# Row loads of the feed-forward chunks issued by GpSimd, and another order of the buffers in the attention loop's scope

## The chip, the core and the metric

The kernel runs on one core of a Trainium2 chip. A core has five engines that the profile tells apart: PE (TensorE, matrix products; PEld is its loading of weights), DVE (VectorE), ACT (ScalarE), POOL (GpSimd) and SP (SyncE, which only issues transfers). Each engine takes its own instructions in order; engines wait for each other by semaphores. A transfer (DMA) is issued by SP, ACT or POOL and lands later. The metric is the device time of one execution in microseconds; of several runs the median counts. All arithmetic is in float32.

## The reference

The input x is a batch of 4 images of 64 x 64 positions with 256 channels. Two layers follow each other:

```python
x = x + L0_conv(_gn(x), ...)       # deformable sampling: 8 groups x 9 taps, bilinear
t = _to_tokens(x)                  # 4 images of 4096 tokens x 256
t = t + L1_attn(_ln_t(t), ...)     # additive attention inside an image
t = t + L1_ffn(_ln_t(t), ...)      # feed-forward of chosen tokens
```

The attention takes `softmax_k(sum_u Wa[u] * tanh(q[i,u] + k[j,u] + bh))` over 32 units for every pair of the 4096 tokens of an image, and the weighted mean of the tokens with it. The feed-forward chooses tokens by a router and leaves the others as they are:

```python
weights = einsum('bsd,do->bso', x, wr) + br
_, idx = top_k(weights, 2048)
sel_idx = idx[:, :2047]
h = gelu(sel @ w1 + b1)            # 256 -> 1024
y = (h @ w2 + b2) * weights[sel]   # 1024 -> 256
return processed + x               # y set at the chosen tokens, 0 elsewhere
```

## The kernel before

**Stages.** First comes the convolution part of all four images together with the sampling of image 0 (L1518 to L1529, to 1355 us of the profiled execution). Then there is a loop over the images n (L1531). In it one scope of buffers (L1538 to L1541) holds three things beside each other: `feed_forward(n - 1)` of the image before, `attention_prep(n)`, and a part of the sampling of image n + 1. They are generators, and the string `turns` (L1547 to L1552), written by hand, says in which order their steps are emitted: m is a step of the feed-forward, o one of the preparation, s one of the sampler. A second scope (L1559 to L1562) holds `attention(n)`, a loop of 8 blocks of 512 queries by 32 blocks of 128 keys by four head parts, with the rest of the sampling as side work. After the loop, `feed_forward(3)` runs alone (L1567).

**What sets the order.** Instructions wrapped in `keep`, and those emitted through `pinned` (DVE in the loop), stay on their engine in the order of the program. Everything else (ACT, SP, POOL and loads) is placed by a scheduler when the kernel is built. The attention loop's order is written out by hand (L1144 to L1150). A buffer is a tile of a pool; the pools of a scope lie one behind the other in each partition of SBUF in the order in which the scope lists them. A pool that lies where pools of an earlier scope lay has to wait for the users of those.

**The feed-forward** (L1367 to L1502). It loads the tokens as `v`, computes router weights, finds the threshold and gives every token a rank. 32 indirect transfers on POOL (L1423, list `put`) scatter the rows, with four numbers behind each (so 260 floats), in the order of rank to `sort_d` in DRAM. While they run, ACT computes the rows of all tokens as if none were chosen (L1435) and sends them to the output (L1439). Then 2048 ranked rows are taken in four chunks of 512. `chunk(s)` (L1449 to L1474) loads them (`get`, L1455, 512 rows of 1,040 bytes), after all of `put`; DVE makes the row numbers `si` (L1461), ACT normalises (L1463), PE transposes (helper `transpose4`, L903 and L904), POOL adds (L1469) and DVE scales (L1471). The body then runs the first product (`ph`, L1483) with gelu on ACT (L1484), the second product (`py`, L1489), DVE's L1492, and for each 128 rows an indirect scatter on POOL to the output (L1496). `chunk(s + 1)` is called after the second of the four scatters of chunk s. The loaded rows are double-buffered inside the one tile `big` (three parts: hT, two xs, two vs), which lies in pool `one` with the weights w1 and w2; the transposed rows (xT) are in pool `row`.

**The start of the attention loop.** `queries(0)` (L998 to L1004) takes two tiles of pool `qp`: it loads qf from DRAM on SP (L1000), and POOL makes qn from it (L1003). PE multiplies keys with qf (D, L1017) and with qn (N, L1027). ACT takes the logarithm of D into a tile r of pool `rp` (L1111) and its exponential (L1113); DVE multiplies it by N (L1032). POOL and DVE add (L1117 to L1124), ACT makes weights (L1039), and PE multiplies them by the values (L1055) into `acv` of pool `ap` (L1079); the weights are in pool `ep`.

**The sampler.** In the stage beside the feed-forward it loads weights `wb` on SP (L819), and DVE multiplies and adds with them (L828, L838). POOL fetches some exact rows by indirect loads `xre` (L679, L684), which DVE uses (L757).

**The preparation.** For each block of keys, PE and ACT (L951, kf) make the factors of the attention; DVE's step `least` (L969) follows in the same block. PE's last instruction of the preparation is L978, after which the attention loop's D can run.

Of the kernel before, what the change touches and what calls it, by code (L numbers as in the profile page):

```python
# [37 lines left out]
PVB = 8  # L38
# [8 lines left out]
def layers_kernel(ctx: ExitStack, tc: tile.TileContext, a, out: bass.AP):  # L47
    nc = tc.nc
# [192 lines left out]
    @contextmanager  # L241
    def scope(*pools):

        with ExitStack() as st:
            for name, bufs, psum in pools:
                kw = {"space": PSUM} if psum else {}
                setattr(S, name, st.enter_context(tc.tile_pool(name=name, bufs=bufs, **kw)))
            yield
            for name, _, _ in pools:
                delattr(S, name)  # L250
# [612 lines left out]
    def sample_any(n):  # L863

        num = nc.values_load(large[0:1, n : n + 1], min_val=0, max_val=L)
        with tc.If(num > P), scope(
            ("smp", 2, 0), ("two", 2, 0), ("sb", 2, 0), ("dn", 1, 0), ("ps_t", 1, 1), ("ps_m", 1, 1)
        ):
            cur = S.two.tile([P, 1], F32, tag="cur", name="cur")
            nc.vector.tensor_copy(cur, part)  # L870
            with tc.For_i(0, NT, 1):
                exact = []
                for _ in exact_rows(n, cur, exact):
                    pass
                put_rows(n, *exact[0])
                nc.vector.tensor_scalar(cur, cur, float(P), None, ALU.add)
# [21 lines left out]
    def transpose4(dst, src, vec=nc.vector):  # L898

        pt = S.ps_d.tile([P, CC, 512], F32, tag="d", name="ptt")  # L900
        for k in range(CC):
            for t in range(4):
                nc.tensor.transpose(pt[:, k, t * P : (t + 1) * P], src[:, t, k * P : (k + 1) * P], ident)  # L903
        vec.tensor_copy(dst, pt)  # L904
# [462 lines left out]
    def feed_forward(n, vec):  # L1367
# [81 lines left out]
        def chunk(s):  # L1449

            o = nh + s % 2 * nx
            xs = big[:, o : o + nx].rearrange("p (t c) -> p t c", t=4)
            o = nh + 2 * nx + s % 2 * nv
            vs = big[:, o : o + nv].rearrange("p (t c) -> p t c", t=4)
            get = nc.sync.dma_start(  # L1455
                out=xs, in_=sort_d[n][s * 512 : (s + 1) * 512].rearrange("(t p) c -> p t c", p=P)
            )
            for ins in put:
                tc.add_manual_dep(get.ins, ins.name, in_order, reason="rows in order")
            si = S.two.tile([P, 4], I32, tag="si", name="si")  # L1460
            vec.tensor_scalar(si, xs[:, :, C + 3], float(n * L), None, ALU.add)  # L1461
            for t in range(4):
                nc.scalar.activation(  # L1463
                    vs[:, t, :], xs[:, t, :C], AF.Identity, bias=xs[:, t, C + 1 : C + 2], scale=xs[:, t, C : C + 1]
                )
            xT = S.row.tile([P, CC, 512], F32, tag="vT", name="xT")
            transpose4(xT, vs, vec)

            nc.gpsimd.tensor_tensor(vs, vs, xs[:, :, :C], ALU.add)  # L1469
            for t in range(4):  # L1470
                vec.scalar_tensor_tensor(  # L1471
                    vs[:, t, :], b2, xs[:, t, C + 2 : C + 3], vs[:, t, :], ALU.mult, ALU.add
                )
            held[s] = xs, vs, si, xT  # L1474

        chunk(0)
        yield
        for s in range(NSORT // 512):
            xs, vs, si, xT = held.pop(s)
            for f in range(FF // P):  # L1480
                ph = S.ps_m.tile([P, 512], F32, tag="pm", name="ph")
                for k in range(CC):
                    nc.tensor.matmul(ph, w1[:, k, rows(f)], xT[:, k, :], start=(k == 0), stop=(k == CC - 1))  # L1483
                S.tables.append(nc.scalar.activation(hT[:, f, :], ph, AF.Gelu_apprx_tanh, bias=b1[:, f, :]))  # L1484
            yield
            for t in range(4):
                py = S.ps_m.tile([P, C], F32, tag="pm", name="py")
                for f in range(FF // P):
                    nc.tensor.matmul(  # L1489
                        py, hT[:, f, rows(t)], w2[:, f, :], start=(f == 0), stop=(f == FF // P - 1)  # L1490
                    )
                vec.scalar_tensor_tensor(  # L1492
                    vs[:, t, :], py, xs[:, t, C + 2 : C + 3], vs[:, t, :], ALU.mult, ALU.add
                )
                m = min(P, NSEL - s * 512 - t * P)
                nc.gpsimd.indirect_dma_start(  # L1496
                    out=out_rows, out_offset=bass.IndirectOffsetOnAxis(ap=si[:m, t : t + 1], axis=0),
                    in_=vs[:m, t, :], in_offset=None,
                )
                if t == 1 and s + 1 < NSORT // 512:  # L1500
                    chunk(s + 1)
                yield  # L1502
# [28 lines left out]
    for n in range(NB):  # L1531
        with scope(("att", 1, 0), ("smp", 2, 0), ("dn", 1, 0)):
            v = S.att.tile([P, NT, C + 1], F32, name="v")
            kf = S.att.tile([P, 2, L], F32, name="kf")

            sampling = sample_image(n + 1) if n + 1 < NB else iter(())
            S.gather = False
            with scope(  # L1538
                ("one", 1, 0), ("two", 2, 0), ("sb", 2, 0), ("row", 2, 0), ("rp", 3, 0),
                ("ps_d", 2, 1), ("ps_n", 1, 1), ("ps_m", 3, 1),  # L1540
            ):  # L1541


                main = feed_forward(n - 1, pinned) if n else iter(())
                prep = attention_prep(n, v, kf, pinned)
                if n:
                    turns = (  # L1547
                        "mos" + "m" * 3 + "mo" * 8 + "om" + "oss" * 2 + "m" + "oss" * 7 + "m" + "oss" * 3
                        + ("m" + "ossss" * 3 + "msss" * 4) * 4
                    )  # L1550
                else:
                    turns = "o" * 10 + "s" + "os" * 24  # L1552
                for turn in turns:
                    next({"m": main, "o": prep, "s": sampling}[turn], None)
                for rest in (main, prep):
                    for _ in rest:
                        pass
            S.gather = True
            with scope(  # L1559
                ("two", 2, 0), ("sb", 2, 0), ("rp", 6, 0), ("qp", 2, 0),  # L1560
                ("ep", 2 * PVB + 1, 0), ("ap", 1, 0), ("ps_d", 2, 1), ("ps_n", 3, 1), ("ps_m", 1, 1),
            ):  # L1562
                attention(n, v, kf, [sampling])
        attention_any(n)
        if n + 1 < NB:
            sample_any(n + 1)
# [39 lines left out]
```

## Time and profile before

| | |
|---|---|
| median of 5 runs | 10437.7 us (10423.64 to 10448.31) |
| profiled execution: time | 10445.84 us |
| profiled execution: span | 10444.1 us |
| granted TensorE clock, mean | 0.934 |
| first attention loop begins (first L1017) | 1468.81 us |
| stage between the loops of images 0 and 1 | 3456 to 3861 us, 405 |
| stage between the loops of images 1 and 2 | 5766 to 6164 us, 398 |
| stage between the loops of images 2 and 3 (no sampling) | 8070 to 8393 us, 323 |
| feed-forward of image 3, alone | 10177 to 10444.1 us, 267 |
| SP ahead of L1455, all waits: for the scatters (`sort`) | 211.0 us in 11 |
| SP ahead of L1455: for `big` | 92.7 us (L263) and 62.2 us (L1492) |
| first L1455 of the four images | 3629.90, 5933.84, 8220.01, 10307.15 |

The span is the time from the first to the last instruction that the profiler shows; the execution's own time is 1.7 us longer. A line of a view names the engine, the line of the program, the operation, and its output and input by the program's names of tiles. In views of waits, `X L1 <- Y Z: a, b, c` says that engine X ahead of its line L1 waited for Y's work on Z, a us in all, in b waits, of which the longest took c. An engine's name with a q (SPq) means its sequencer, the part that issues. In the order of time a line begins with the start and the duration in us, and the bracket behind it gives the idle time of the engine ahead of that instruction and what ended it. The page's strip of 40 digits shows the busy share of an engine in slices of a fortieth of the span, in tenths. The profile is of one execution; durations below a microsecond vary between instances.

### The profile page before, as it was taken

The numbers are of one execution on the slowest core, as the hardware profiler recorded it, in microseconds if no ns is written. First come the engines' busy times: TensorE is split into PE (matmuls) and PEld (weight loads), VectorE is DVE, ScalarE is ACT, GpSimd is POOL, SyncE is SP. The second block draws the span as 40 slices with busy tenths as digits, with TensorE's granted clock in tenths as the row PEclk, the third lists the DMA queues.
The fourth block names the chain that finished last, engine by engine and source line by source line (L and its number), as shares of the span: only waits on it lengthen the run. The fifth ranks groups of instructions, "written<-read, shape, count | busy, mean of one in ns | idle before, by whom it ended". The sixth has DMA issues, their size and how long they took to land. (4 is left out here: it accounts for less than half of the span.)

```text
span 10444.1 us, 117382 instructions
## 1 busy us (share of the span) xinstructions
PE 9292.6 (89%) x38892; PEld 4517.1 (43%) x38892; DVE 8527.5 (82%) x13743; ACT 7465.7 (71%) x8525; POOL 5226.6 (50%) x3042
## 2 busy tenths in 40 slices
PE   5777779999999589999999589999999699999995
PEld 3444434444444344444444344444444344444443
DVE  5798979898989679899898679899898367777772
ACT  3333348888888338888888358888887389999991
POOL 0231027676555327677655237677555155555552
PEclk9788879999999789999999789999999799999997
DMA  3476632222222342222111442222111300000002
GB/s 106 138 201 188 206 122 64 62 65 61 71 66 72 122 148 54 52 53 56 53 58 44 139 136 54 53 52 55 52 58 39 103 13 8 10 7 7 7 5 76
DMA packets 381592, 766.07 MB, mean 73 GB/s; under 512 B 49361, under 2 KB 212849, under 8 KB 380945
## 3 DMA queue, kind: packets, MB, share of 16 engines
q1 hardware_dynamic: 290448, 608.84, 18.8%
q0 software_dynamic: 30144, 45.87, 3.0%
q10 hardware_dynamic: 60352, 103.50, 2.8%
q8 instruction: 312, 5.11, 0.2%
q14 instruction: 336, 2.74, 0.1%
HBM read 580.88 MB, written 177.14 MB: 73 GB/s over the span
## 5 line engine op out<-in xcount | busy, mean ns | idle before, releaser
L1032 DVE TENSOR_TENSOR r<-nn,r 128x512 f32<-128x512 f32 x6144 | 3937.7, 681 | 874.1 <-PE nn L1027 819.3
L1027 PE MATMUL nn<-qn,kf 32*128 32x512 f32 (+1 forms) x12288 | 4518.0, 640 | 133.9 <-DVE r L1032 97.3
L1117 POOL TENSOR_TENSOR r<-r 128x1024 f32<-128x1024 f32 x1024 | 2708.7, 2645 | 2647.8 <-DVE r L1032 2637.9
L1111 ACT ACTIVATE r<-d 128x1024 f32<-128x1024 f32 x3072 | 3114.0, 1014 | 1095.0 <-DVE r L1121 701.5
L1017 PE MATMUL d<-qf,kf 32*128 32x512 f32 (+1 forms) x12288 | 3340.3, 632 | 76.5 <-DMA qf<-qf 43.1
L1113 ACT ACTIVATE r<-r 128x1024 f32<-128x1024 f32 x3072 | 3124.1, 1051 | 32.7
L1027 PEld LDWEIGHTS nn<-qn,kf 32*128 32x128 f32 (+1 forms) x12288 | 1400.0, 185 | 1898.4 <-DVE r L1032 1448.3
L1055 PE MATMUL pv<-v,et 128*128 128x257 f32 x8192 | 2116.5, 402 | 14.8 <-DVE acv L1079 14.8
L1055 PEld LDWEIGHTS pv<-v,et 128*128 128x128 f32 x8192 | 1516.0, 195 | 981.4 <-issue 771.5
L1017 PEld LDWEIGHTS d<-qf,kf 32*128 32x128 f32 (+1 forms) x12288 | 1018.2, 186 | 1340.3 <-issue 725.6
L1119 POOL TENSOR_TENSOR r<-r 128x512 f32<-128x512 f32 x1024 | 1331.7, 1300 | 99.4 <-DVE r L1032 24.3
L828 DVE TENSOR_TENSOR prd<-xs,wb 128x1024 f32<-128x1024 f32 x768 | 978.0, 1273 | 90.6 <-DMA wb<-wt 83.8
L838 DVE TENSOR_TENSOR ac<-ac,prd 128x1024 f32<-128x1024 f32 x768 | 993.3, 1293 | 6.6
L724 POOL DMA_INDIRECT ga<-tab,tii x576 | 701.5, 1218 | 348.9 <-DVE so L738 203.4
L1039 ACT ACTIVATE et<-et,nshift 128x512 f32<-128x512 f32 x1024 | 723.7, 707 | 29.6 <-DVE et L1124 29.6
L1121 DVE TENSOR_TENSOR r<-r 128x512 f32<-128x512 f32 x1024 | 719.7, 703 | 4.1 <-POOL r L1117 3.7
L1124 DVE TENSOR_TENSOR et<-r 128x512 f32<-128x512 f32 x1024 | 695.6, 679 | 0.4
L263 PE MATMUL pc<-xn,diag 128*128 128x512 f32 x1008 | 449.2, 601 | 21.4 <-ACT xn L397 8.3
L788 POOL TENSOR_TENSOR xr<-xr,outb 128x512 f32<-128x512 f32 x64 | 87.1, 1367 | 551.5 <-DMA xr<-in_x_dram 551.4
L263 PE MATMUL ptc<-ident,xp 128*128 128x128 f32 (+1 forms) x576 | 136.0, 349 | 207.4 <-ACT tb L456 206.2
L263 PEld LDWEIGHTS pc<-xn,diag 128*128 128x128 f32 x1008 | 190.7, 192 | 255.6 <-issue 221.7
L456 ACT COPY tb<-ptc 128x256 f32<-128x256 f32 (+1 forms) x288 | 104.4, 370 | 240.5 <-PE ptc L263 131.0
(342 smaller groups left out, 5253.5 us busy)
## 6 DMA issues: line engine op xcount, KB each, us to landing
wb<-wt SPq DMA_DIRECT2D x800, 512.0 KB
tab<-tb ACTq DMA_DIRECT2D x128, 256.0 KB
v<-t SPq DMA_DIRECT2D x64, 512.0 KB
xs<-xp SPq DMA_DIRECT2D x32, 680.0 KB
xp<-xp ACTq DMA_DIRECT2D x32, 544.0 KB
xt<-in_x_dram SPq DMA_DIRECT2D x32, 512.0 KB
xr<-in_x_dram SPq DMA_DIRECT2D x64, 256.0 KB
t<-xr SPq DMA_DIRECT2D x64, 256.0 KB
```

Source lines behind the costliest of these rows:

```text
L263: return lambda *args, **kw: keep(op(*args, **kw))
L828: keep(nc.vector.tensor_tensor(pr.rearrange("p (r w) -> p r w", w=W), src, wb.rearrange("p (r w) -> p r w", w=W), ALU.mult,))
L838: keep(nc.vector.tensor_add(ac[:, f, :], ac[:, f, :], pr))
L1017: keep(nc.tensor.matmul(d[:, j, :], kf[g, blk, rows(kt)], qs[q][0][g, blk, :], start=True, stop=True))
L1027: keep(nc.tensor.matmul(nn, kf[g, blk, rows(kt)], qs[q][1][g, blk, :], start=True, stop=True))
L1032: keep(nc.vector.tensor_tensor(r[:, j, :], ns[j], r[:, j, :], ALU.mult))
L1039: keep(nc.scalar.activation(ets[b], ets[b], AF.Exp, bias=nshift))
L1055: keep(nc.tensor.matmul(pv, ets[b0 + i][:, rows(j)], v[:, k0 + i, :], start=(i == 0), stop=(i == PVB - 1)))
L1111: keep(nc.scalar.activation(rs[b, p], ds.pop((b, p)), AF.Ln))
L1113: keep(nc.scalar.activation(rs[b, p], rs[b, p], AF.Exp, scale=-1.0))
L1117: keep(nc.gpsimd.tensor_tensor(rs[b, 1], rs[b, 1], rs[b, 2], ALU.add))
L1119: keep(nc.gpsimd.tensor_tensor(rs[b, 1][:, 0], rs[b, 1][:, 0], rs[b, 3][:, 0], ALU.add))
```

## The change

Two edits. The load of the ranked rows of each chunk, L1455, is issued by GpSimd in place of SyncE: 16 loads in the whole program, four for each image. And the scope of the attention loop lists its pools in another order: `ep` comes straight after `sb`, `rp` after it, then `ap`, and `qp` last of the pools in SBUF; before, it was `rp`, `qp`, `ep`, `ap`. Their sizes are as before, and the pools of PSUM (`ps_d`, `ps_n`, `ps_m`) are not touched.

```diff
@@ -1452,7 +1452,7 @@
             xs = big[:, o : o + nx].rearrange("p (t c) -> p t c", t=4)
             o = nh + 2 * nx + s % 2 * nv
             vs = big[:, o : o + nv].rearrange("p (t c) -> p t c", t=4)
-            get = nc.sync.dma_start(
+            get = nc.gpsimd.dma_start(
                 out=xs, in_=sort_d[n][s * 512 : (s + 1) * 512].rearrange("(t p) c -> p t c", p=P)
             )
             for ins in put:
@@ -1557,8 +1557,8 @@
                         pass
             S.gather = True
             with scope(
-                ("two", 2, 0), ("sb", 2, 0), ("rp", 6, 0), ("qp", 2, 0),
-                ("ep", 2 * PVB + 1, 0), ("ap", 1, 0), ("ps_d", 2, 1), ("ps_n", 3, 1), ("ps_m", 1, 1),
+                ("two", 2, 0), ("sb", 2, 0), ("ep", 2 * PVB + 1, 0), ("rp", 6, 0), ("ap", 1, 0), ("qp", 2, 0),
+                ("ps_d", 2, 1), ("ps_n", 3, 1), ("ps_m", 1, 1),
             ):
                 attention(n, v, kf, [sampling])
         attention_any(n)
```

## The prediction

> **What bounds the kernel now.** I read the page first, then busy times by stage, then the waits inside the stages that the change touches, then the order in time.
>
> ```profile
> span 10444.1 us, 117382 instructions
> PE 9292.6 (89%) x38892; PEld 4517.1 (43%) x38892; DVE 8527.5 (82%) x13743; ACT 7465.7 (71%) x8525; POOL 5226.6 (50%) x3042
> PE   5777779999999589999999589999999699999995
> DVE  5798979898989679899898679899898367777772
> ```
>
> PE and DVE are full in four long plateaus, the attention loops. Between them lie four stages that are not full: feed-forward of one image beside the preparation of the next (images 1, 2, 3 of the loop over images, counted from 0), and the last feed-forward alone. The change touches only these. The busy times by stage (length; then PE, PEld, DVE, ACT, POOL) show the first one and the last one:
>
> ```profile
> 3456.00:3861.00 405.00, 248.62 (x816) 154.54 (x816) 272.00 (x537) 105.18 (x152) 84.51 (x66) 0.76 0.51 163
> 10177.00:10444.10 267.10, 150.16 (x540) 101.59 (x536) 73.35 (x258) 54.52 (x89) 63.10 (x56) 0.77 0.22 74
> ```
>
> No engine is full there, so waits set their length: 405 + 398 + 323 + 267 = 1393 us of 10444, the most that is in question. Two waits are the change's subject. The first, in the waits of SP and of all engines from 3596 to 3650 us (total, times, longest):
>
> ```profile
> SPq L1455 <- DMA sort<-v,rif: 29.9, 3, 27.5
> ACT big L1463 <- DMA big<-sort: 31.0, 2, 30.4
> DVE prd L828 <- DMA wb<-wt: 29.1, 3, 27.5
> ```
>
> The 32 scatters of L1423 run to 3628.1 (32 x 1.264 us from 3585.25). Chunk 0's load L1455 stands in SP's queue until they have landed (3629.90), and the sampler's wb loads stand behind it, so DVE idles 27.5 us for wb. Beside it ACT idles 30.4 us for the same rows: its next instruction is chunk 0's L1463. Image 2 repeats this (28.5 and 32.3 us).
>
> The second, in order of time at the start of image 1's loop:
>
> ```profile
> 3846.22 2.55 POOL L1496 DMA_INDIRECT out_dram<-big,si  x1 [4.42 <-DMA out_dram<-big,si]
> ...
> 3856.43 0.55 SPq L1000 DMA_DIRECT2D qf<-qf  x1
> ...
> 3857.13 1.00 POOL L684 DMA_INDIRECT xre<-in_x_dram,rii  x1 [8.36 <-DMA out_dram<-big,si]
> ...
> 3860.58 2.09 PE L1017 MATMUL d<-qf,kf 32*128 32x512 f32 x8 [13.61 <-DMA qf<-qf]
> ...
> 3862.82 1.94 ACT L1111 ACTIVATE r<-d 128x1024 f32<-128x1024 f32 x2 [52.69 <-PE d L1017]
> ...
> 3863.97 0.42 DVE L757 TENSOR_TENSOR tte<-xre,outb 128x256 f32<-128x256 f32 x1 [16.45 <-ACT r L1111]
> ...
> 3868.14 1.29 DVE L1032 TENSOR_TENSOR r<-nn,r 128x512 f32<-128x512 f32 x2 [2.37 <-PE nn L1027]
> ```
>
> The last scatter of the feed-forward lands 10 us after its issue. Only then does SP load qf (3856.43), PE multiply (3860.58), ACT start (3862.82), DVE follow (3868.14). A look at L1111 alone shows that ACT has a wait of its own that ends at the same landing, 3856.3, and a later one for d, 3862.7:
>
> ```profile
> L1111 ACTq EVENT_SEMAPHORE x2: 38/3216/6394, 3856.3 to 3862.7; - x2
> ```
>
> **Part 1, qp last in the scope.** It adds no instruction; it moves buffers. Bytes per partition in images 1 and 2, from where both scopes start: the feed-forward's `one` takes 0 to 54,240, `sb` ends at 73,312, `row` at 81,504, `rp` at 93,792. The loop's qp lies at 36,992 to 53,376 before (inside `one`, over w1 and w2) and at 75,920 to 92,304 after (over `row` and `rp`). That qf waits for the scatters though it overlaps w1 alone shows that a buffer waits for every user of a pool that it overlaps. In its new place it waits for the last L1483 (done 3808) and the qe stores (last issued 3799.4), so qf is loaded some 40 us early, and d of the first key block is in PSUM when PE has done L978 (3846.97). The two qn products of L1003 (1.57 us each) move ahead too; POOL has holes of 3.7 to 4.6 us between L1496, which hide them. Image 3 has the same overlaps.
>
> What is late next: the six r buffers of rp move to 47,232 to 71,808, still over the end of `one`, so L1111 keeps its wait to 3856.3. It gains 3862.82 - 3856.5 = 6.3 us, not 14. In images 1 and 2 DVE has L757 ahead of L1032. If L757 stayed at 3863.97, L1032 would start when L838 ends, 3865.8, and gain 2.3 us (2.0 in image 2). xre landed 6.8 us after its issue with two 512 KB qf loads beside it; indirect rows land in a median of 2.6. Without those loads I take 5 us, between 2 and 6.3. Image 3 has no L757: its landing is 8388.4, L1111 8394.86, so 6.3. Image 0 has no wait (qf loaded at 1415.6, d follows L978 at once): 0. **Sum 16.3 us, between 10.6 and 18.9.**
>
> **Part 2, the 16 loads on POOL.** Removed from SP: 16 issues of 0.37 us and the waits ahead of them. Added to POOL: the same issues and waits. POOL has nothing of use to do between the last L1423 and L1469 (20 us idle), so its own waiting for the rows costs nothing in chunks 0 and 1.
>
> Gain: wb flows, and DVE takes up L828 at 3608 instead of 3635.8. It does not win 27.5 us. After 7.7 us of work (3635.81 to 3643.53) it stands at `least`, which needs ACT's kf (L951), and ACT still stands at chunk 0's rows. From these, ACT's next four groups take 2.07 + 1.00 + 2.08 + 1.02 = 6.2 us, so `least` starts at 3633.78 + 6.3 = 3640.1 instead of 3643.53: 3.4 us earlier per image, if the rows come as before.
>
> Price: let d be how much later a load lands. The trace has no plain load on POOL. The nearest row is L1423: 128 rows of 1,040 bytes take POOL 0.96 us, against 0.37 on SP; a load has 512 such rows. POOL also acted 0.7 us after SP on one landing (3857.13, 3856.43). So d is between 0.7 + 0.6 = 1.3 and 0.7 + 4 x 0.96 - 0.37 = 4.2. I take 2.0, nearer the row. The lower end excludes a gain in the load itself, except that two wb loads no longer run beside it. Images 1 and 2 win 2 x (3.4 - d). In image 3 and at the end no sampler runs and the chain goes through chunk 0's rows (ACT L1463 waits 16.5 and 62.0 us): -2d. Chunks 2 and 3 there: ACT waited only 0.5 us for chunk 2, but has 1.03 us idle before each following L1484, which covers most; I charge a quarter of d each, -4 x d/4. In images 1 and 2 DVE's sampling steps (DVE busy 42 and 48 of 50 us) cover chunks 2 and 3. Part 2 is 6.8 - 5d = -3.2 us.
>
> [...] SP's row shows one queue held for 27.5 us. [...]
>
> **Sum.** 16.3 - 3.2 = 13.1 us. The profiled execution took 10445.84 (span 10444.1 and 1.7 around it), 8 us over the median; 10445.84 - 13.1 = 10432.7 for a like one, 10437.7 - 13.1 = 10424.6 for the median. Own range: 18.9 + 6.8 - 6.5 = 19.2 won to 10.6 + 6.8 - 21 = 3.6 lost, 10418.5 to 10441.3.
>
> **Rivals.** A, faster: DVE's 27.5 us really go. Only pinned instructions keep their order; ACT's L1463 may be placed anew when POOL loads. If prep's next qe and kf came ahead of it, ACT and DVE would both work through the sort. For it: one prep block takes 15.7 us (kf at 3641.63 and 3657.28), and two would fit. Against: the rows are due when they were. Price: up to 27.5 - 3.4 = 24 us more per image; at half of that, 10424.6 - 24 = 10400.
>
> B, slower than before: POOL's queue is in order, and the loads of chunks 2 and 3 are placed behind L1496, each of which waits 4 to 5 us for the landing of the one before. A load then lands 4.2 + 5.6 us late, and ACT's slack covers 3.8: 6 us on four loads, 24; with 8.4 for chunk 0 and 1.6 in images 1 and 2, less 16.3, it is 18 us slower, 10455. It decides once those four loads cost over some 3 us each at d = 2. Against it: in the shown order L1496 follows its row within 1.5 us of the old load.
>
> C, part 1 doesn't do what it says: another user of `row` or `rp` keeps qf late. Part 2 remains: 10437.7 + 3.2 = 10441.
>
> **Numbers.** Forecast 0.46, A 0.33, B 0.14, C 0.07. A measurement here tells 0.2% (21 us) from no change. Faster by that: most of A, 0.30. Slower: most of B, 0.10. Within: 0.60. The range leaves out the lower part of A and the upper part of B: 10390 to 10452.
>
> **What would show it.** Part 1: qf issued near 3810 instead of 3856, L1111 straight after the last L1496 lands, waiting for that landing and no longer for d; the idle of L1017 before qf gone. Part 2: no SP wait at L1455; wb loads between 3600 and 3630; DVE idle before `least` for ACT, not before L828; L1463 idle 30 us plus d. I am wrong if L1111 comes no earlier, if ACT's order around L1463 is new, if L1463 in the last feed-forward waits over 4 us longer than 62, or if an engine idles for L1496.

## The result, and the profile after

The changed kernel takes 10446.9 us (median of 24 runs, 10424.77 to 10458.15), the kernel before 10437.21 us (44 runs). The ratio is 1.0008, 95% interval 1.0002 to 1.0014: 8 us slower, between 2 and 15. The forecast was 13 us faster.

The page of the changed kernel, the lines that answer to those shown of before, and its line for the DMA queue of GpSimd:

```profile
span 10435.5 us, 117354 instructions
PE 9294.2 (89%) x38892; PEld 4515.4 (43%) x38892; DVE 8525.7 (82%) x13743; ACT 7464.8 (72%) x8525; POOL 5232.9 (50%) x3058
q0 software_dynamic: 32448, 54.39, 3.3%
```

The busy times have not moved. POOL has 16 instructions more, and 8.5 MB have moved to its queue (45.87 MB before): the 16 loads. This profiled execution lies 10 us under the median of its kernel, that of before 9 us over, so their spans differ the wrong way. So I compare stage by stage; the rest of the span, almost all of it the loops, differs by 16 us between these two executions (us, one profile each):

| | before | after | difference |
|---|---|---|---|
| first L1423 to last L1496, beside image 1 / 2 / 3 | 261.0 / 260.2 / 199.1 | 260.7 / 264.0 / 199.9 | -0.3 / +3.8 / +0.8 |
| last L1496 to the 101st L1032 of image 1 / 2 / 3 | 144.7 / 141.9 / 131.6 | 146.2 / 147.6 / 127.3 | +1.5 / +5.7 / -4.2 |
| last feed-forward, first L1423 to the end | 179.5 | 179.7 | +0.2 |
| all of these | 1318.0 | 1325.4 | +7.3 |
| the rest of the span | 9126.0 | 9110.2 | -15.9 |

So the stages that the change touches together got 7.3 us longer in this pair, about what the medians differ by. One pair does not prove it: beside images 1 and 2 a stage varies by 6 us and more between profiles of kernels that treat it alike (see e7 and e8). But the starts of the loops of images 1 and 2 got longer, where 5 us each had been forecast as won, and that is traced below instruction by instruction.

The busy times of the first stage and the last one (length; PE, PEld, DVE, ACT, POOL; granted clock, DMA share, GB/s) are within 2% of those before, but for POOL, 91.34 in place of 84.51 and 65.86 in place of 63.10:

```profile
3453.00:3858.50 405.50, 251.06 (x818) 154.04 (x814) 270.36 (x537) 105.04 (x152) 91.34 (x71) 0.76 0.52 164
10167.54:10435.54 268.00, 149.87 (x536) 101.62 (x536) 72.83 (x257) 53.59 (x88) 65.86 (x60) 0.77 0.22 74
```

The waits around the scatters of image 1, 3592 to 3646 us (total, times, longest):

```profile
ACT big L1463 <- DMA big<-sort: 32.6, 1, 32.6
DVE least L263 <- ACT kf L951: 28.7, 2, 28.4
DVE prd L828 <- DMA wb<-wt: 2.9, 2, 1.5
POOL big L1455 <- DMA sort<-v,rif: 2.6, 1, 2.6
```

SP has no wait at L1455 any more and wb flows: DVE's wait for it fell from 29.1 to 2.9 us. But DVE now stands 28.4 us at `least`, as forecast, and ACT stands 32.6 us for the rows, 2.2 more than before.

The start of the loop of image 1, in order of time (start, duration, in brackets the idle time and what ended it):

```profile
3802.52 1.41 SPq L1000 DMA_DIRECT2D qf<-qf  x2
...
3842.45 2.57 POOL L1496 DMA_INDIRECT out_dram<-big,si  x1 [3.18 <-DVE prd L828]
...
3845.98 2.09 PE L1017 MATMUL d<-qf,kf 32*128 32x512 f32 x8
...
3853.90 1.07 POOL L684 DMA_INDIRECT xre<-in_x_dram,rii  x1 [5.57 <-DMA out_dram<-big,si]
...
3859.42 0.43 DVE L757 TENSOR_TENSOR tte<-xre,outb 128x256 f32<-128x256 f32 x1 [12.81 <-issue]
...
3859.94 0.14 DVE L263 CAST wide<-lo 1x1 int32<-1x1 f32 x1
...
3860.31 1.94 ACT L1111 ACTIVATE r<-d 128x1024 f32<-128x1024 f32 x2 [55.85 <-DMA tr<-t]
...
3865.62 1.89 DVE L1032 TENSOR_TENSOR r<-nn,r 128x512 f32<-128x512 f32 x3 [4.41 <-PE nn L1027]
```

qf is loaded 54 us earlier and D runs at once. Yet L1111 does not start when the scatter has landed (3853.9, where L684 takes up), but 6.4 us later, 0.2 us after `wide<-lo` on DVE. That step belongs to the preparation; it stands behind L757 in DVE's queue, and L757 waits for xre. In image 3, which has no L757, the same step comes early, and L1111 follows the landing:

```profile
8370.63 2.55 POOL L1496 DMA_INDIRECT out_dram<-big,si  x1 [2.40 <-DVE lo L263]
8370.84 0.14 DVE L263 CAST wide<-lo 1x1 int32<-1x1 f32 x1
...
8382.00 1.94 ACT L1111 ACTIVATE r<-d 128x1024 f32<-128x1024 f32 x2 [23.10 <-DMA out_dram<-big,si]
```

### The profile page after: what moved, and what is told of

Read it like the earlier page. It is cut to its first block, busy times and chain, and to the rows that moved or that the text cites. A ratio compares the mean times of both kernels' runs of the same rounds, so it can differ in the third digit from the quotient of the medians.

```text
span 10435.5 us, 117354 instructions
## 1 busy us (share of the span) xinstructions
PE 9294.2 (89%) x38892; PEld 4515.4 (43%) x38892; DVE 8525.7 (82%) x13743; ACT 7464.8 (72%) x8525; POOL 5232.9 (50%) x3058
## 3 DMA queue, kind: packets, MB, share of 16 engines
q1 hardware_dynamic: 282000, 600.32, 18.6%
q14 instruction: 336, 2.75, 0.1%
## 5 line engine op out<-in xcount | busy, mean ns | idle before, releaser
L1032 DVE TENSOR_TENSOR r<-nn,r 128x512 f32<-128x512 f32 x6144 | 3938.3, 681 | 868.5 <-PE nn L1027 813.9
L1111 ACT ACTIVATE r<-d 128x1024 f32<-128x1024 f32 x3072 | 3114.0, 1014 | 1090.3 <-DVE r L1121 704.8
L263 PE MATMUL pc<-xn,diag 128*128 128x512 f32 x1008 | 448.7, 601 | 22.2 <-ACT xn L397 8.3
L1423 POOL DMA_INDIRECT sort<-v,rif x128 | 132.5, 1035 | 291.0 <-DVE rif L263 174.7
```

Source lines behind the costliest of these rows:

```text
L263: return lambda *args, **kw: keep(op(*args, **kw))
L1032: keep(nc.vector.tensor_tensor(r[:, j, :], ns[j], r[:, j, :], ALU.mult))
L1111: keep(nc.scalar.activation(rs[b, p], ds.pop((b, p)), AF.Ln))
```

## The experiments

The table gives from each profile the time in us from the issue of the last L1496 to the first L1111 and to the first L1032 in images 1, 2 and 3, and the ratio of the kernel's time to that of the kernel before on the same chip. The theories and rivals that the texts name are those of the expectation quoted there.

| kernel | to L1111 | to L1032 | ratio (95%) |
|---|---|---|---|
| before | 16.6 / 17.1 / 17.8 | 21.9 / 22.0 / 22.8 | |
| after | 17.9 / 17.9 / 11.4 | 23.2 / 23.2 / 16.7 | 1.0008 (1.0002 to 1.0014) |
| e1 part 1 alone | 17.8 / 18.2 / 11.1 | 23.1 / 23.5 / 16.5 | 0.9997 (0.9987 to 1.0006) |
| e2 part 2 alone | 16.8 / 16.9 / 17.7 | 22.1 / 22.2 / 22.7 | 1.0004 (0.9996 to 1.0013) |
| e3 part 1, rp stays | 11.1 / 10.7 / 11.1 | 19.6 / 19.1 / 16.4 | 0.9989 (0.9980 to 0.9999) |
| e4 part 1, `lo` apart | 11.0 / 11.2 / 11.1 | 18.7 / 18.3 / 16.4 | 0.9987 (0.9977 to 0.9998) |
| e5 e3, 128 rows | 3.1 / 2.6 / 2.7 | 11.5 / 10.7 / 7.1 | 0.9969 (0.9957 to 0.9981) |
| e6 loads on ACT | 16.7 / 17.0 / 17.8 | 21.9 / 22.3 / 23.1 | 1.0017 (1.0008 to 1.0026) |
| e7 chunks 0, 1 on POOL | 16.8 / 17.1 / 18.0 | 22.1 / 22.4 / 23.3 | 1.0010 (1.0001 to 1.0020) |
| e8 chunks 2, 3 on POOL | 16.7 / 17.3 / 17.6 | 22.0 / 22.6 / 22.9 | 1.0004 (0.9995 to 1.0014) |
| e9 change, rp stays | 10.7 / 10.6 / 11.1 | 18.8 / 18.6 / 16.4 | 1.0006 (0.9997 to 1.0015) |
| e10 before, 128 rows | 8.8 / 8.8 / 9.0 | 14.1 / 14.1 / 14.2 | 0.9974 (0.9965 to 0.9983) |
| e11 e5, early xre | 3.1 / 2.5 / 2.7 | 8.4 / 7.8 / 8.0 | 0.9969 (0.9960 to 0.9978) |
| e12 e3, 112 rows | 3.2 / 2.7 / 2.8 | 11.6 / 11.0 / 8.1 | one run |
| e13 e11, loads on POOL | 3.6 / 3.1 / 2.7 | 8.9 / 8.4 / 7.8 | 0.9972 (0.9963 to 0.9981) |
| e14 e11, loads on ACT | 6.1 / 2.5 / 2.6 | 11.4 / 7.4 / 8.0 | 0.9977 (0.9967 to 0.9987) |
| e15 e11, whole change | 3.1 / 3.2 / 2.7 | 8.4 / 8.5 / 7.6 | 0.9977 (0.9967 to 0.9986) |
| e16 e11 again | 3.6 / 2.6 / 2.7 | 8.9 / 7.9 / 7.6 | 0.9961 (0.9948 to 0.9975) |

**e1, part 1 alone** (after, with `nc.sync.dma_start` at L1455).

> Only the new order of the pools; the loads are on SP as before. Measure: from the issue of the last L1496 to the first L1032 of the loop, in images 1, 2, 3: 21.9, 22.0, 22.8 us before; 23.2, 23.2, 16.7 after. Theory W (a new wait takes the place of the old one): the tiles r now lie over the old pool `two`, and L1111 waits for the tile `lo` in it, whose last DVE steps stand behind L757, which waits for xre. Then it is 23, 23, 16.7 again, qf is loaded early and helps in image 3 alone; in all some 3 to 4 us faster at these places, less 2 us per image that the start of the loop gives back: time within 5 us of before. Rival P (the loss is all in the loads on POOL): without them L1111 starts when the last L1496 has landed, 17 us in all three images, and the time is about 15 us under before.

The start times are those of after: the loss at the starts belongs to part 1. Rival P falls.

**e2, part 2 alone** (before, with `nc.gpsimd.dma_start` at L1455).

> Only the loads on POOL; pools in the old order. Theory W: the starts of the loops are as before (21.9, 22.0, 22.8 us); the loads cost 1.2 us each in chunk 0 and more in chunks 2 and 3, where they stand behind L1496 on POOL; from the first L1423 to the last L1496 images 1, 2, 3 and the last feed-forward lose 0 to 4 us each, 4.5 in all: time 3 to 7 us over before. Rival P: the whole loss of 8 us and more, since part 1 gains 15 by it: 20 us or more over before.

The starts are those of before. The time is 4 us over before, with an interval from 4 under to 14 over: as theory W expected, and not 20.

**e3, another place for rp** (on e1).

```diff
-("two", 2, 0), ("sb", 2, 0), ("ep", 2 * PVB + 1, 0), ("rp", 6, 0), ("ap", 1, 0), ("qp", 2, 0),
+("two", 2, 0), ("sb", 2, 0), ("rp", 6, 0), ("ep", 2 * PVB + 1, 0), ("ap", 1, 0), ("qp", 2, 0),
```

> Loads on SP; qp last in the scope as in the change, but rp stays in its old place straight after sb, over pool `one` alone. Theory W: L1111 waits for the landing of the last L1496 and no longer for `lo` or for d; L1032 then follows L757, some 17.5 us after the issue of the last L1496 in images 1 and 2 and 16.7 in image 3, against 22: 13 to 15 us won at these places, and the time 8 to 15 us under before. Rival P: as e1, no difference between the two. If L684 or another instruction holds L1111 in both, 23 us again.

L1111 now starts 11 us after the issue in all three images, and the kernel is 11 us faster than before, in an interval from 1 to 21: the lower end of what had been forecast for part 1 (10.6 to 18.9).

**e4, one small tile apart** (on e1; the traces of both have the same order of instructions on DVE, ACT and POOL and the same order of loads).

```diff
-        lo = S.two.tile([1, 2], F32, tag="lo", name="lo")
+        lo = S.att.tile([1, 2], F32, name="lo")
```

> As e1 (new order of the pools, loads on SP), but the tile `lo` of two floats is taken from pool att, which lives through the loop, in place of pool `two`. The order of instructions on every engine is that of e1. Theory W: that one wait goes, L1111 starts at the landing of the last L1496, some 10.5 us after its issue, and L1032 some 17.5 us after it in images 1 and 2: 5 us per image less than e1. If another user of `two` or `sb` holds r: as e1, 23 us. Rival P: as e1 in any case.

This names the wait. The start of the loop of image 1, first in e1, then in e4:

```profile
3845.85 2.57 POOL L1496 DMA_INDIRECT out_dram<-big,si  x1 [4.71 <-DMA out_dram<-big,si]
...
3862.74 0.43 DVE L757 TENSOR_TENSOR tte<-xre,outb 128x256 f32<-128x256 f32 x1 [15.59 <-DMA xre<-in_x_dram,rii]
3863.26 0.14 DVE L263 CAST wide<-lo 1x1 int32<-1x1 f32 x1
3863.63 1.94 ACT L1111 ACTIVATE r<-d 128x1024 f32<-128x1024 f32 x2 [56.99 <-DMA xr<-in_x_dram]
```

```profile
3846.04 2.57 POOL L1496 DMA_INDIRECT out_dram<-big,si  x1 [4.44 <-DMA out_dram<-big,si]
...
3856.99 1.94 ACT L1111 ACTIVATE r<-d 128x1024 f32<-128x1024 f32 x2 [50.87 <-DMA out_dram<-big,si]
...
3863.06 0.42 DVE L757 TENSOR_TENSOR tte<-xre,outb 128x256 f32<-128x256 f32 x1 [15.72 <-DMA xre<-in_x_dram,rii]
3863.58 0.14 DVE L263 CAST wide<-lo 1x1 int32<-1x1 f32 x1
3864.78 1.87 DVE L1032 TENSOR_TENSOR r<-nn,r 128x512 f32<-128x512 f32 x3
```

With the eight bytes of `lo` out of pool `two`, ACT starts 6.6 us earlier, straight after the landing. The profile of e1 puts the wait down to a load (`xr<-in_x_dram`); it was `lo`. Then DVE's own L757 is next: L1032 follows it at 18.7 us.

**e5, 128 rows in the last scatter** (on e3).

```diff
+        keeps = S.one.tile([P, 1], F32, name="keeps")
+        vec.tensor_scalar(keeps, ident[:, P - 1 :], 0.5, None, ALU.is_lt)
...
-            vec.tensor_scalar(si, xs[:, :, C + 3], float(n * L), None, ALU.add)
+            vec.tensor_scalar(si, xs[:, :, C + 3], float(n * L), None, ALU.add); wl = xs[:, 3, C + 2 : C + 3]; s < 3 or vec.tensor_mul(wl, wl, keeps)
...
-                m = min(P, NSEL - s * 512 - t * P)
+                m = P
```

> As e3, and the last scatter of each feed-forward writes 128 rows in place of 127: the weight of the one row more is set to 0, so that the row gets the value that it has already (one small DVE product per image). In all kernels so far the last L1496 takes POOL 2.55 us and lands after 11 us, the others take 0.96 and land after 2.4 to 5. Theory N (the 127 rows make it slow): it lands after 3 to 5 us, L1111 starts 5 to 6 us after the issue of the last L1496 in place of 11, L1032 in images 1 and 2 12 to 14 us after it in place of 19, and the program ends 7 to 8 us after its last L1496 in place of 14.4: some 24 us under e3. Rival (the last one is slow because it is the last, whatever its size): 11 us again, time as e3.

Theory N holds. The start of the loop of image 1 in e5:

```profile
3832.16 1.05 POOL L1496 DMA_INDIRECT out_dram<-big,si  x1 [4.31 <-DMA out_dram<-big,si]
...
3833.02 2.09 PE L1017 MATMUL d<-qf,kf 32*128 32x512 f32 x8
...
3835.27 1.94 ACT L1111 ACTIVATE r<-d 128x1024 f32<-128x1024 f32 x2 [42.57 <-PE d L1017]
...
3841.91 0.43 DVE L757 TENSOR_TENSOR tte<-xre,outb 128x256 f32<-128x256 f32 x1 [8.27 <-DMA xre<-in_x_dram,rii]
```

The scatter costs POOL 1.05 us in place of 2.75 in e3, and the last thing that L1111 waits for is d. The program ends 4.98 us after its last L1496 (14.36 before). The kernel is 32 us faster than before (20 to 45), e3 was 11; most of the 32 should come from here, and e10 tests that.

**e12, 112 rows** (on e3: `m = 112` for the last scatter).

> As e3, and the last scatter of each feed-forward writes 112 rows in place of 127: 15 chosen rows of each image keep the value of a row not chosen, so this part of the result is left out. If a count of rows that 16 does not divide makes a scatter slow: POOL takes about 0.96 us for it, it lands after 2.4 to 4 us, and L1111 starts 3 us after its issue, as in e5. If any count under 128 does: 2.5 us and about 10 us, as in e3.

```profile
3833.31 1.17 POOL L1496 DMA_INDIRECT out_dram<-big,si  x1 [4.76 <-DMA out_dram<-big,si]
...
3836.55 1.94 ACT L1111 ACTIVATE r<-d 128x1024 f32<-128x1024 f32 x2 [40.50 <-PE d L1017]
```

Not every count under 128 is slow: with 112 rows L1496 takes POOL 1.17 us and L1111 starts 3.2 us after its issue, with 127 (e3) 2.75 and 11.1. The traces also show how 127 and 128 rows differ. At the end of the program nothing runs beside the last scatter; these are the rates from its issue to the end of the span, in slices of a fortieth, and the packets, first of before (14.4 us), then of e5 (5.0 us; 48 of the 49 packets are the scatter's):

```profile
GB/s 0 0 0 0 0 0 0 0 0 5 15 16 16 26 0 0 11 23 23 23 23 34 23 23 34 23 23 23 20 0 0 0 0 0 0 0 0 0 0 0
DMA packets 528, 0.14 MB, mean 10 GB/s; under 512 B 496, under 2 KB 496, under 8 KB 528
```

```profile
GB/s 0 0 0 0 0 0 0 0 0 0 0 0 328 295 360 66 0 0 0 0 0 0 0 0 0 0 0 0 0 0 0 66 0 0 0 0 0 0 0 0
DMA packets 49, 0.14 MB, mean 28 GB/s; under 512 B 16, under 2 KB 16, under 8 KB 48
```

With 128 rows the data are 32 packets of 4 KB, up to 18 of them under way at once, and all are through within 0.5 us. With 127 rows there are again 32 packets of data, but never more than two under way at once, so they take 6.8 us, from 3.6 to 10.4 us after the issue; 480 packets of 12 or 16 bytes come before and beside the first of them (3.2 to 5.0 us), which 128 rows do not have. Three counts were run, 112, 127 and 128; why the packets of 127 rows go at most two at a time, none of them shows.

**e10, 128 rows in the kernel before.**

> The kernel before with the last scatter of 128 rows alone (pools in the old order, loads on SP). Theory N: the scatter lands 3 to 5 us after its issue; qf is loaded then, L1017 follows some 4.5 us later, L1032 14 to 17 us after the last L1496 in place of 22, the end of the program 5 us after it in place of 14.4: 24 to 30 us under before. Then the order of the pools is worth only the rest to e5, 5 to 10 us. If e5's gain came from both together and not from the scatter, less than 15 us under before.

27 us faster (18 to 36): the scatter gives most of e5's 32 alone. What the pools still give at the starts (14.1 against 11 us) is small beside it.

**e11, early xre** (on e5).

```diff
-        xr = S.sb.tile([P, C], F32, tag="xr", name="xre")
+        xr = S.dn.tile([P, C], F32, tag="tte", name="xre")
...
-        tt = S.dn.tile([P, C], F32, tag="tte", name="tte")
+        tt = xr
```

> As e5, and the rows xre are loaded into the tile tte of pool dn, which lives through both stages, and are added to in place; so L684 needs no buffer that the feed-forward had, and stands ahead of the scatters on POOL. Theory W: L757 was what held DVE, and `lo`, at the start of the loops of images 1 and 2; without it L1032 comes 7 to 8 us after the last L1496 there, as in image 3, in place of 11: 6 to 8 us under e5, 10390. If DVE is held by something else, 11 us again and the time of e5.

```profile
3835.15 1.06 POOL L1496 DMA_INDIRECT out_dram<-big,si  x1 [4.41 <-DMA out_dram<-big,si]
...
3836.99 0.14 DVE L263 CAST wide<-lo 1x1 int32<-1x1 f32 x1
3838.26 1.94 ACT L1111 ACTIVATE r<-d 128x1024 f32<-128x1024 f32 x2 [41.71 <-DVE ac L838]
...
3843.57 1.29 DVE L1032 TENSOR_TENSOR r<-nn,r 128x512 f32<-128x512 f32 x2 [5.30 <-PE nn L1027]
```

No L757 stands there any more, and images 1 and 2 start as image 3 does. This version beats both kernels: 0.9969, and 0.9961 in e16. Its gain over e5 (3 us at two starts) is smaller than the times can tell, and the 6 to 8 us that were expected do not show in them.

**e7 and e8, the loads divided.** `(nc.gpsimd if s < 2 else nc.sync)` at L1455 in e7, the reverse in e8.

> Loads of chunks 0 and 1 on POOL, those of chunks 2 and 3 on SP; pools in the old order. Theory W: images 3 and last keep the whole price of part 2 (199.6 and 166.5 us from the first L1423 to the last L1496), image 2 loses its price (261 in place of 263.9). Rival B of the prediction, in images 3 and last too (loads of chunks 2 and 3 behind L1496): 198.2 and 165.4 there.

> Loads of chunks 2 and 3 on POOL, those of chunks 0 and 1 on SP; pools in the old order. Theory W: images 3 and last as with SP, 198.2 and 165.4 us; image 2 keeps the price of chunk 3 behind L1496, 263.5; image 1 between 261 and 262. Rival (image 2's loss comes from chunk 0): image 2 261.

From the first L1423 to the last L1496 beside image 3, nine profiles with loads on SP lie at 197.3 to 199.7 us, five with all loads on POOL at 199.3 to 200.4. e7 has 196.1, e8 200.8: in image 3 theory W has it the wrong way round, and the prediction's rival B is right there, as far as one profile of each can tell. The whole waits of ACT for rows beside image 3, first e7, then e8:

```profile
ACT big L1463 <- DMA big<-sort: 17.5, 3, 16.9
```

```profile
ACT big L1463 <- DMA big<-sort: 22.9, 3, 16.3
```

In e8 each of the chunks 2 and 3 makes ACT wait 3.3 us, in the whole change 3.5 and 3.9 (0.2 and 0.3 in e7); the load is placed behind an L1496 and takes POOL 0.8 us. In the last feed-forward both differ little from the whole change (167.2 and 166.5, against 166.3 in the mean). Beside images 1 and 2 the nine profiles themselves spread over 6 and 7 us (257.0 to 263.0, 259.5 to 266.5), so a single e7 and e8 decide nothing there. By time e7 is 10 us over before (1 to 21) and e8 4 (5 under to 15 over).

**e6, loads on ACT.** `nc.scalar.dma_start` at L1455.

> Loads on ACT's queue, pools in the old order: SP is as free for wb as with the loads on POOL, POOL as free as before. Measure: from the first L1423 to the last L1496, images 1, 2, 3 and the last feed-forward: 261.2, 260.9, 198.2, 165.4 us (mean of four kernels with loads on SP), 261.3, 263.9, 199.6, 166.5 (mean of two with loads on POOL). Theory W (the price is POOL's: 1.2 us more per load, and a place behind L1496; the gain of the free SP is given back, since the 32 scatters last 3 us longer beside the wb loads): images 3 and last as with SP, 198.2 and 165.4, images 1 and 2 261 or up to 2 us less, the scatters 45 us long as with POOL. Rival Q (SP's waiting was worth more, and POOL's price hides it): images 1 and 2 3 to 10 us less.

The scatters took 45.1 and 44.0 us, as they do with POOL, and images 1, 2, 3 and last 256.8, 263.6, 200.2 and 164.6 us: in sum what SP has, but image 3 is over all nine profiles with SP, where 198.2 had been expected. The time is 18 us over before (8 to 27). The stages of the one profile do not show where.

**e9, the change with rp in its old place.**

> The whole change, except that rp stays straight after sb (the pools of e3, the loads on POOL). Theory W: starts of the loops as in e3 (L1111 11 us after the last L1496 in all three images, L1032 19, 19, 16.4), the feed-forward stages as in the change; so the two parts add, and the time is 10 to 14 us under the changed kernel, 2 to 8 under before. If the loads on POOL spoil the start of the loop by themselves (L684 late), L1032 comes 22 us and more after it in images 1 and 2.

The starts came as expected, and the touched stages sum to 1314.4 us, 11 under after and 4 under before. The time does not follow: 6 us over before (3 under to 16 over), where 2 to 8 under had been expected. The expectation is missed, though the interval just reaches its near end.

**e13 to e16, the price of part 2 on the faster kernel.**

> e11 (no wait for the 127 rows, xre early, rp straight after sb), with the loads on POOL. Theory W (price of part 2 is 1.1 us per first load, scatters 2.4 us longer in images 1 and 2, less some 3 us each that DVE and ACT win there): 2 to 5 us over e11, and in the profile image 3 and last 1 to 2 us longer from the first L1423 to the last L1496. Rival T (part 2 costs more than the stages show, as the times of e7 and e9 hint): 10 us and more over e11.

> e11 with the loads on ACT's queue. Theory W: within 3 us of e11. Rival T (a load off SP costs more than the stages show, as the time of e6 hints): 10 to 17 us over e11.

> The whole change (its order of pools, the loads on POOL) together with the scatter of 128 rows and the early xre. Theory W: with L757 early, `lo` is done early, and the place of rp over pool `two` costs nothing: L1111 2.5 to 3.2 us after the last L1496, L1032 8 us after it, time as e13. If the place of rp has a price of its own: L1111 later than that, and 5 us and more over e13.

> e11 once more, on the chip of e13 to e15, so that they are compared on one chip: about 0.9965 of before.

e15 against e13: the place of rp has no price that shows once `lo` is early. e13, e14 and e15 against e16 are 11, 17 and 17 us slower, in intervals of 9 to 14 us to either side; rival T is nearer, but not separated from W. 3.5 us of it are at the end of the program in e13 and e15 (8.3 and 8.8 us after the last L1496, 5.0 in e16). Another 2.7 us are in image 2, where POOL issues chunk 0's load 4.9 and 5.0 us after the last L1423, and 2.2 to 2.3 us after it in after, e2 and e9; the profile does not show what it waits for.

## Why the prediction was wrong

**Part 1 failed at one step: "What is late next."** The text put the six r buffers at 47,232 to 71,808, "still over the end of `one`, so L1111 keeps its wait to 3856.3". Its own list of bytes has `one` end at 54,240 and `sb` at 73,312: the r buffers also lie over pool `two` and most of `sb`. In the old place they lay over `one` alone. So L1111 got a wait for every user of `two`, the last of which is `lo`, behind L757, behind xre, behind the landing. The prediction looked at L757 only as work that DVE does ahead of L1032, not as something that ACT can come to wait for through a buffer. Shown by e1 and e4, which differ in that tile alone: 17.8 and 11.0 us to L1111. The prediction's own sign of being wrong, that L1111 comes no earlier, came in images 1 and 2: 17.9 us after the issue in both, against 16.6 and 17.1.

The sizes, from the last L1496 to the 101st L1032, in means over the profiles with old pools (before, e2, e6, e7, e8), the change's pools (after, e1) and rp in place (e3, e9): image 1 143.8, 146.2, 140.5; image 2 144.8, 147.7, 141.6; image 3 132.8, 126.3, 125.9. The change's order loses 2.4 and 3.0 and wins 6.5: 1.2 won in place of 16.3. With rp in place it is 13.4. The term for image 3 (6.3) was right, and the mechanism for qf (issued at 3802, D at once) too. The 5 us for images 1 and 2 would have come out as 3.3.

**Part 2 went as forecast in sign, and cost more.** Forecast was -3.2 us. In means over nine profiles with loads on SP and five on POOL, first L1423 to last L1496 grew by 1.9, 1.8, 1.9 and 1.0 us (images 1, 2, 3, last): 6.6. The mean of image 3 is clear of the scatter; those of images 1 and 2 are not, since profiles of one kind differ there by 4 to 11 us. Three terms were off:

- d, taken as 2.0, is 0.6 to 1.4 for chunk 0: from the end of the last L1423 to L1463 it takes 5.5, 5.7 and 6.5 us with SP, 6.5, 7.1 and 7.0 with POOL (images 1, 3 and last, means). A load holds POOL 0.8 us. With 1.1 in place of 2.0 the text's 6.8 - 5d would have been some 1 us won. So the miss is in the next two, and that the sign came out right was luck: a d too large made up for part of a gain that was not there.
- "If the rows come as before": they do not. With SP free, wb loads run beside the scatters; the 32 of them take 45.6 and 44.3 us in place of 43.9 and 42.3 (means, images 1 and 2; 40.2 in image 3, where nothing is sampled). And `least` had less than 3.4 us to gain. The sum put ACT's four groups end to end, 6.2 us, but ACT's kf waits for PE's pk, which waits for qe (L958), and it did so before too (lines below). Before, kf was done at 3642.65, so that `least` at 3643.53 could come only 0.9 us earlier, not 3.4. From L1463 to `least` it took 7.9 us in after, 9.8 before.
- Chunks 2 and 3, charged at a quarter of d: ACT waits 3 us more for each in image 3, as rival B said (e8, and after itself).

The kf of image 1, first before, then after:

```profile
3641.63 1.02 ACT L951 ACTIVATE kf<-pk 128x1024 f32<-128x1024 f32 x1 [2.19 <-PE pk L950]
```

```profile
3641.42 1.02 ACT L951 ACTIVATE kf<-pk 128x1024 f32<-128x1024 f32 x1 [1.69 <-PE pk L950]
```

The free queue of SP did take 26 us off DVE's wait for wb (29.1 to 2.9), and in the sum nothing was won: DVE stood as long, 28.4 us, at the next thing, `least`.

What the loads on POOL cost in time stays open between 4 us (e2 against before) and 17 (e15 against e16; e9 against e3 gives 18, on two chips). With 1.2 won in part 1 and 6.6 lost in part 2 the stages give 5 us slower; measured are 2 to 15.

Rival A did not come: ACT still stands at chunk 0's rows (32.6 us), with kf behind. Rival C did not come: qf was early. Two small sums of the text do not come out, and nothing else rests on them: 32 x 1.264 us from 3585.25 would end at 3625.7, while the trace has the last L1423 start at 3627.1 and end at 3628.1; and rival B's own terms turn to a loss at 3.8 us per load, not at 3.

## What to carry to other kernels

A pool that is moved to free one buffer moves its neighbours: list for every pool of the scope, old place and new, all the pools that it overlaps and their last user on each engine, however small the tile. Eight bytes with a user in a queue that waits for a transfer held ACT 6.6 us here (e1 against e4). Before shuffling what waits for a slow transfer, ask why it is slow: here 128 rows in place of 127 were worth 27 us alone (e10), and part 1 with rp in its old place 11 (e3).

## What the runs showed of the hardware

A scatter of 127 rows landed 10.2 to 11.2 us after its issue (before, after, e6, e7, e8) and took POOL 2.55 us or a little more. In its place, where nothing runs beside it, 128 rows took POOL 0.96 us and landed after 2.4 (e5), and 112 rows took 0.94, with L1111 2.8 us after the issue (e12). The slow one stood in four places of this kernel, and the trace of before had it: the prediction quotes the 10 us and, for indirect rows, the median of 2.6 without asking for the difference. A plain load of 512 rows holds POOL 0.8 us and SP's queue 0.37 in the median. With the loads on POOL and 128 rows, the end of the program came 8.3 and 8.8 us after the last scatter (e13, e15), against 5.0 (e5, e16); with 127 rows it came 12.8 to 13.3 after it (after, e2, e9), against 14.4. Why, no run tells.
